# A sparse two-layer graph kernel: the first two same-lane slots summed ahead of TensorE, the bias as a matmul, and sorting held back

## The chip, the core and the metric

The kernel runs on one core of a Trainium2 chip. The core has five engines that run in parallel, each with its own queue of instructions in fixed order: TensorE (PE; its weight loads are listed apart as PEld), VectorE (DVE), ScalarE (ACT), GpSimd (POOL) and SyncE (SP). They wait for one another through semaphores. Data come from and go to the main memory by DMA, which SP, ACT and POOL issue. The metric is the device time of one execution in microseconds (us), as the median of several executions.

## What is computed

Two layers over a graph of 4096 nodes with 512 features. `adj` is a 4096 x 4096 matrix with some eight entries off the diagonal per row and a diagonal, all between 0.05 and 1; `x` is 4096 x 512.

```python
# layer 0
a = adj + I
d = sum(a, axis=1) ** -0.5
support = (d[:, None] * a * d[None, :]) @ x
h = layernorm(x + relu(support @ W.T + b))
# layer 1: attention over the entries of adj, with a mask value of 1e16
adj1 = maximum(adj, I)
scores = (q @ k.T) * kd ** -0.5 + 0.01 * I - 1e16 * (1 - adj1)
out = layernorm(h + softmax(scores) @ v @ Wo)       # 8 heads, summed
```

Where all entries of `adj` lie below 1, the mask leaves every row of layer 1 its own node alone, so that layer 1 is `layernorm(h + h @ Wv @ Wo)`, one product with a combined weight matrix `wvo`. The kernel tests this on the chip (`test`) and has a general path for the other case, which these inputs don't enter.

## The kernel before, in words

The 4096 rows are cut into NT = 32 tiles of 128. `few_edges_below_one` has two stages.

**First stage** (the loop from L1015). Each turn loads one 128 x 4096 tile of `adj` (2 MB), three turns ahead, over SP's queue; ScalarE sums its rows (`sum_rows`, L694) for the degree, GpSimd makes d from it (`scaling`, L706 to L709), TensorE transposes a tile of x and multiplies it by `wT` (`times`, L687), ScalarE scales the product by d (`keep_y`, L720) and GpSimd writes it to `y` in main memory. At the side VectorE turns each tile into a list of edges, a generator of small steps (`steps`) of which every turn takes RATE = 7 (`some`). A tile has 16 long steps, 8 MAX8 (L749) and 8 FIND_INDEX8 (L750), each over 512 columns: the eight largest entries of each eighth of a row and where they stand. Then some 30 short instructions (`short`) sort the 64 candidates of a row into at most 24 edges, with column and weight; those of one tile are mixed among the long steps of the next. `match` then moves the edges, over TensorE and a permutation, so that each row has KH = 9 slots (`cols_all`, `wr_all`).

EARLY = 12 tiles are scanned while they pass in the first stage, and their degree comes from the candidates (L935) and not from ScalarE. The last five tiles stay resident. The remaining 15 pass by once for their row sums in a small pool (`a_n`) and are loaded a second time in the second stage (`reload`) to be scanned. `order` is early, resident, again.

**Second stage** (the loop from L1246, tiles in `order`). For tile i and each slot k, GpSimd issues an indirect DMA that gathers the 128 rows of `y` that the edges name (`gather`, L1077) into a buffer `g`, 18 slots ahead of their use, in 19 buffers. ScalarE builds a 128 x 128 matrix per slot (`spread`) with the weights at the right places, and TensorE multiplies: nine products into one PSUM tile (`zs[i]`, L1280). In the first SAME = 5 slots every row keeps its lane, so that their matrices are one and the same 0/1 matrix (`s_t[:, KH]`, L983) times a weight per row (L986); the other four have one each (L973, L977). For the last two tiles (SUMMED) the five same-lane slots are summed first: ScalarE scales the first gathered tile by its weight (L1094), VectorE adds the others (`presum`, L1096), and one product with the 0/1 matrix takes the place of five (L1104).

VectorE then does `own_bias` (yo = yo * own + b, L1139, yo being the tile's own rows of `y`), `scaled` (h = zs * d + yo, L1146) and `residual` (relu and + x, L1154); ScalarE takes squares for the norms (L1162); TensorE transposes h (L673) two tiles later and multiplies by `wvo`; ScalarE scales by the last norm and issues the write of the result (L1185). The remaining scan and sort steps are dealt out over the first SPREAD = 28 tiles of this stage. ScalarE checks reloaded and resident tiles for negative entries, half a tile at a time (`scan_half`, L699); a reload waits for buffers that these halves and VectorE's scan set free. On SP's queue the reloads stand between the loads of `yo` and x, which wait for `scaled` and `residual` of three tiles before.

The order on each engine isn't that of the program text: a scheduler places the instructions, and the order is fixed when the program is built.

Of the kernel before, what the change touches and what calls it, by code (L numbers as in the profile page):

```python
# [419 lines left out]
def few_edges_below_one(  # L420
# [47 lines left out]
    recs = ctx.enter_context(tc.tile_pool(name="recs", bufs=8))  # L468
# [84 lines left out]
    EARLY, LAG = 12, 5  # L553
# [21 lines left out]
    b_bc = const.tile([P, D], FP, name="b_bc")  # L575
    wvo = const.tile([P, ND, D], FP, name="wvo")

    def transpose_w():
        for dc in range(ND):
            pt = ps_t.tile([P, 512], FP, name="pt")  # L580
            for oc in range(ND):
                nc.tensor.transpose(pt[:, ts(oc, P)], w_nat[:, oc, ts(dc, P)], ident)
            nc.scalar.copy(wT[:, dc, :], pt[:, :D])

# [143 lines left out]
    def extraction(t, a_t, rec):  # L728
# [6 lines left out]
        idx = keys.tile([P, C], U32, name="idx")  # L735
# [9 lines left out]
        long = []  # L745
        for s in range(SEGS):
            o = slice(s * E, (s + 1) * E)
            seg = a_t[:, ts(s, SW)]
            long.append(lambda o=o, seg=seg: nc.vector.max(v[:, o], seg))  # L749
            long.append(lambda o=o, seg=seg: nc.vector.max_index(idx[:, o], v[:, o], seg))  # L750
# [13 lines left out]
        def drop(f, r):  # L764
# [42 lines left out]
            [one(rec[:, 2], w, 0.0, row1n, op0=ALU.is_gt, op1=ALU.mult)],  # L807
# [7 lines left out]
        return long, short  # L815
# [103 lines left out]
    def steps():  # L919

        after = [[] for _ in range(STEPS)]
        for n, t in enumerate(order):
            if t not in a_tiles:
                reload()
            edges[t] = dict(rec=recs.tile([P, 7, K], FP, name="rec"))
            long, short = extraction(t, a_tiles[t], edges[t]["rec"])
            begun.append(t)
            for j in range(STEPS):
                long[j]()
                for f in after[j]:  # L930
                    f()
                if j == STEPS - 1:
                    picked.append(t)
                    if t in early:
                        nc.vector.tensor_reduce(  # L935
                            deg_all[:, t : t + 1], v_all[:, t, :], AX.X, ALU.add
                        )
                yield
            after = [[] for _ in range(STEPS)]
            for j, fs in enumerate(short):  # L940
                after[j] += fs
            after[len(short)].append(lambda t=t: sorted_.append(t))
        for fs in after:
            for f in fs:
                f()
            yield
# [19 lines left out]
    def spread(t, s_t, k, alone=False):  # L966


        wr = wr_all[:, t]

        def away():
            sq = mat.tile([P, P], FP, name="sq")
            nc.scalar.activation(sq, cols1, AF.Square, bias=wr[:, 2, k : k + 1])  # L973
            return sq

        if k >= SAME:
            nc.scalar.activation(  # L977
                s_t[:, k, :], away(), AF.Relu,
                scale=wr[:, 3, k : k + 1], bias=wr[:, 1, k : k + 1],
            )  # L980
            return
        if k == 0:
            nc.scalar.activation(s_t[:, KH, :], away(), AF.Relu, scale=-1.0, bias=1.0)  # L983
        if alone:
            return
        nc.scalar.activation(s_t[:, k, :], s_t[:, KH, :], AF.Copy, scale=wr[:, 1, k : k + 1])  # L986
# [4 lines left out]
    RATE = 7  # L991
# [21 lines left out]
    nc.gpsimd.dma_start(b_bc, bcast_rows(b0, D))  # L1013
    setup, left = iter(()), None
    for t in range(NT + 1):  # L1015
# [16 lines left out]
        for j in [j for at, j in due if at == t and j in early]:  # L1032
            scaling(j)
# [35 lines left out]
    SUMMED = (NT - 2, NT - 1)  # L1069
    slots = {}  # L1070
# [29 lines left out]
    def summed_products(i, pos, c=slice(0, D)):  # L1100

        k = SAME + pos if pos < KH - SAME else None
        g = slots[i * KH if k is None else i * KH + k]
        nc.tensor.matmul(  # L1104
            zs[i][:, c], mats[i][:, KH if k is None else k, :], g[:, c],
            start=(pos == 0), stop=(k is None),
        )

    def build(count):

        for _ in range(count):
# [5 lines left out]
            spread(order[i], mats[i], k, i in SUMMED)  # L1117
# [19 lines left out]
    def own_bias(i):  # L1137
        own = own_all[:, order[i] : order[i] + 1]
        nc.vector.scalar_tensor_tensor(yo[i], yo[i], own, b_bc, op0=ALU.mult, op1=ALU.add)  # L1139
# [3 lines left out]
    def scaled(i, c=slice(0, D)):  # L1143
        if i not in hs:
            hs[i] = p2.tile([P, D], FP, name="h", bufs=3)
        nc.vector.scalar_tensor_tensor(  # L1146
            hs[i][:, c], zs[i][:, c], d_all[:, order[i] : order[i] + 1], yo[i][:, c],
# [42 lines left out]
    def test():  # L1190
# [32 lines left out]
        [(i, k) for i in range(NT) for k in range(KH) if not (i in SUMMED and 0 < k < SAME)]  # L1223
# [22 lines left out]
    for i in range(NT + 2):  # L1246
        if i < NT:
            zs[i] = ps_a.tile([P, D], FP, name="acc")
        free = len([t for t in scanned if t in picked])
        p = i - 1  # L1250
        has_p = 0 <= p < NT
        for k in range(KH):
# [7 lines left out]
            if i == NT - 1:  # L1260
# [8 lines left out]
                if k == 8:  # L1269
                    for n in range(KH - SAME + 1):  # L1270
# [8 lines left out]
            elif i < NT:  # L1279
                nc.tensor.matmul(  # L1280
                    zs[i], mats[i][:, k, :], slots.pop(i * KH + k),
                    start=(k == 0), stop=(k == KH - 1),
# [4 lines left out]
            if i + 1 in SUMMED and k >= KH - SAME:  # L1287
                presum(i + 1, k - (KH - SAME))
# [26 lines left out]
            if k == 6 and i < NT:  # L1315
                own_bias(i)
# [48 lines left out]
```

## Time and profile before

| what | before |
|---|---|
| median of 3 runs | 649.07 us (648.53 to 650.29) |
| the profiled execution's own time | 647.33 us |
| its span, first to last instruction | 645.5 us |
| granted TensorE clock, mean | 0.944 of full speed |
| moved by DMA | 222.14 MB, mean 344 GB/s |
| gathers (L1077) | 288, 977 ns each on GpSimd, 7.3 us from issue to landing |
| products with gathered tiles (L1280) | 540 instructions for 270 products |
| scan (L749, L750) | 512 instructions, 687 and 691 ns each |
| own rows and bias (L1139) | 32, 743 ns each |
| matrices by scaling the 0/1 matrix (L986) | 150, 394 ns each |

The span is what the profiler saw between the first and the last instruction; the execution's own time has 1.8 us around it. Busy times are sums over an engine's records; on VectorE and ScalarE these overlap a little, so that the distance from one start to the next is the better measure of what an instruction costs in a full stretch.

### The profile page before, as it was taken

What the parts mean: (1) busy time and instruction counts of PE and PEld (TensorE: products, weight loads), DVE (VectorE), ACT (ScalarE), POOL (GpSimd) and SP (SyncE); (2) the same over time, 40 slices, a digit from 0 to 9 for tenths busy, and PEclk for the clock granted to TensorE, in tenths of its full rate; (3) what the DMA queues carried; (4) which work ended last, traced back from release to release, by engine and by line L of the source; (5) the groups of instructions that cost most, each with busy time, mean ns of one, the idle gap of its engine ahead of it and who ended that gap; (6) DMA issues with size and microseconds to landing.
All of it is one profiled execution on the core that took longest, in us unless ns stands there. A gap on an engine that the chain in (4) does not pass through costs nothing. (4 is left out here: it accounts for less than half of the span.)

```text
span 645.5 us, 7946 instructions
## 1 busy us (share of the span) xinstructions
PE 556.8 (86%) x1604; PEld 258.0 (40%) x1604; DVE 543.6 (84%) x2141; ACT 509.1 (79%) x1121; POOL 351.2 (54%) x464
## 2 busy tenths in 40 slices
PE   1698696888689486999999989999999999999794
PEld 1344342444244132444443434444444444444352
DVE  5679999999999994999999979999999996532431
ACT  1868888779779775999898957999979989994433
POOL 5132421323232377767666757766767777777700
PEclk9599998799879886999999989999999999999798
DMA  8999999999999289999999898999999988888721
GB/s 332 391 427 422 428 421 426 424 421 422 422 428 395 102 263 366 340 411 408 399 401 405 324 391 302 380 382 360 365 404 341 340 268 272 292 270 253 243 70 54
DMA packets 51850, 222.14 MB, mean 344 GB/s; under 512 B 8080, under 2 KB 9104, under 8 KB 45520
## 3 DMA queue, kind: packets, MB, share of 16 engines
q1 hardware_dynamic: 18416, 119.55, 45.6%
q0 software_dynamic: 28240, 92.56, 40.8%
q10 hardware_dynamic: 5136, 9.44, 3.8%
q14 instruction: 43, 0.35, 0.2%
q8 instruction: 15, 0.25, 0.2%
HBM read 204.73 MB, written 16.78 MB: 343 GB/s over the span
## 5 line engine op out<-in xcount | busy, mean ns | idle before, releaser
L1077 POOL DMA_INDIRECT g<-y,cols_all x288 | 281.4, 977 | 112.6 <-issue 41.9
L1280 PE MATMUL acc<-g,s_t 128*128 128x512 f32 x540 | 258.1, 612 | 23.8 <-DMA g<-y,cols_all 13.4
L749 DVE MAX8 v_all<-a_t 128x8 f32<-128x512 f32 x256 | 172.7, 687 | 16.9 <-DMA a_t<-in_adj_dram 16.9
L750 DVE FIND_INDEX8 idx<-v_all,a_t 128x8 uint32<-128x512 f32 x256 | 175.9, 691 | 0.0
L1280 PEld LDWEIGHTS acc<-g,s_t 128*128 128x128 f32 x540 | 98.0, 194 | 140.9 <-issue 92.8
L687 PE MATMUL acc<-wT,xT 128*128 128x512 f32 x256 | 126.6, 647 | 24.1 <-ACT xT L678 24.0
L699 ACT ACTIVATE dump<-a_t 128x2048 uint8<-128x2048 f32 (+1 forms) x52 | 119.5, 2299 | 4.4 <-DMA a_t<-in_adj_dram 4.3
L687 PE MATMUL acc<-wvo,hT 128*128 128x512 f32 x256 | 118.6, 606 | 5.0 <-ACT hT L678 4.6
L687 PEld LDWEIGHTS acc<-wT,xT 128*128 128x128 f32 x256 | 51.1, 207 | 86.9 <-issue 58.1
L687 PEld LDWEIGHTS acc<-wvo,hT 128*128 128x128 f32 x256 | 49.7, 196 | 67.4 <-issue 58.1
L973 ACT ACTIVATE sq<-cols,wr_all 128x128 f32<-128x128 f32 x160 | 58.1, 396 | 0.3 <-ACT hT L678 0.2
L694 ACT ACTIVATE dump<-a_n 128x4096 uint8<-128x4096 f32 x15 | 54.4, 3628 | 4.7 <-DMA a_n<-in_adj_dram 4.6
L977 ACT ACTIVATE s_t<-sq,wr_all 128x128 f32<-128x128 f32 x128 | 57.6, 487 | 0.5
L550 POOL DMA_DIRECT2D x_t<-in_x_dram x32 | 18.0, 562 | 68.1 <-PE pt L673 67.5
L986 ACT ACTIVATE s_t<-s_t,wr_all 128x128 f32<-128x128 f32 x150 | 48.9, 394 | 0.0
L1146 DVE SCALAR_TENSOR_TENSOR h<-acc,d_all,yo 128x512 f32<-128x512 f32 (+1 forms) x33 | 24.0, 727 | 20.9 <-PE acc L1280 15.9
L762 DVE MAX8 top<-key 128x8 f32<-128x64 f32 x192 | 41.0, 221 | 0.5
L678 ACT COPY hT<-pt 128x512 f32<-128x512 f32 x31 | 17.9, 579 | 23.8 <-PE pt L673 22.8
L706 POOL TENSOR_SCALAR deg<-deg_all 128x1 f32<-128x1 f32 x32 | 6.8, 224 | 48.0 <-ACT dump L694 47.9
L1139 DVE SCALAR_TENSOR_TENSOR yo<-yo,own_all,b_bc 128x512 f32<-128x512 f32 x32 | 23.8, 743 | 7.7 <-ACT own_all L1135 7.7
L673 PE MATMUL pt<-ident,x_t 128*128 128x128 f32 x128 | 20.3, 291 | 8.8 <-DVE above L841 7.6
L765 DVE MATCH_REPLACE8 key<-top,key 128x64 f32<-128x64 f32 x128 | 27.2, 214 | 0.0
(128 smaller groups left out, 643.5 us busy)
## 6 DMA issues: line engine op xcount, KB each, us to landing
a_t<-in_adj_dram SPq DMA_DIRECT2D x30, 2048.0 KB, 17.2
a_n<-in_adj_dram SPq DMA_DIRECT2D x15, 2048.0 KB, 17.4
x_t<-in_x_dram POOLq DMA_DIRECT2D x32, 256.0 KB, 11.9
yo<-y SPq DMA_DIRECT2D x32, 256.0 KB, 5.3
x_t<-in_x_dram SPq DMA_DIRECT2D x32, 256.0 KB, 5.6
out_dram<-r_t ACTq DMA_DIRECT2D x32, 256.0 KB, 6.4
g<-y,cols_all POOLq DMA_INDIRECT x288, 7.3
y<-y_t POOLq DMA_DIRECT2D x17, 256.0 KB, 11.9
```

Source lines behind the costliest of these rows:

```text
L687: nc.tensor.matmul(u, srcT[:, dc, :], w[:, dc, :], start=(dc == 0), stop=(dc == ND - 1))
L694: nc.scalar.activation(dump[:, : part.shape[1]], part, AF.Copy, accum_out=dst)
L699: nc.scalar.activation(dump[:, o], a_t[:, o], AF.Relu, scale=-1.0, accum_out=neg_all[:, t, halves[0] : halves[0] + 1],)
L749: long.append(lambda o=o, seg=seg: nc.vector.max(v[:, o], seg))
L750: long.append(lambda o=o, seg=seg: nc.vector.max_index(idx[:, o], v[:, o], seg))
L762: return lambda: nc.vector.max(top[:, f, r * 8 : r * 8 + 8], keyf[:, f])
L765: return lambda: nc.vector.match_replace(keyf[:, f], top[:, f, r * 8 : r * 8 + 8], keyf[:, f], 0.0)
L973: nc.scalar.activation(sq, cols1, AF.Square, bias=wr[:, 2, k : k + 1])
L977: nc.scalar.activation(s_t[:, k, :], away(), AF.Relu, scale=wr[:, 3, k : k + 1], bias=wr[:, 1, k : k + 1],)
L986: nc.scalar.activation(s_t[:, k, :], s_t[:, KH, :], AF.Copy, scale=wr[:, 1, k : k + 1])
L1077: nc.gpsimd.indirect_dma_start(out=slots[j], out_offset=None, in_=y[:, :], in_offset=bass.IndirectOffsetOnAxis(ap=cols_all[:, t, k : k + 1 ...
L1280: nc.tensor.matmul(zs[i], mats[i][:, k, :], slots.pop(i * KH + k), start=(k == 0), stop=(k == KH - 1),)
```

## The change

Four things, with what they bring along:

- *Two same-lane slots summed in tiles 1 to 29* (`summed`). ScalarE scales the first gathered tile by its weight, VectorE adds the second times its weight, and one product with the 0/1 matrix does for both. The two scaled matrices aren't built. Tile 0 stays as it was, and so do the last two tiles with five summed slots.
- *Bias on TensorE*. b is split into three bfloat16 parts that add up to it (`split_b`), and each tile begins with a small matmul of a 3 x 128 tile of ones with these (`bias`), which starts the sum in PSUM. For this the weights are multiplied by d as they are sorted (`one(w, w, d_all...)`), since zs is no longer scaled afterwards, and `scaled` becomes h = yo * own + zs. `own_bias` is gone.
- *Held sorting*. `extraction` is cut into `scan` (the long steps) and `sorting` (the short ones). Tiles wait in a list: the first five sorts run with the third to seventh scan (n = 2 to FULL = 6), none with n = 7 to 17, and from n = HELD = 18 on two with each scan until the list is empty. The index tiles get 15 buffers for this, the edge records 5 instead of 8.
- *Early tiles and rate*. EARLY is 14 instead of 12, so 13 tiles are reloaded instead of 15, and the first stage takes 9 steps a turn instead of 7. d of an early tile is computed as soon as its scan ends.

```diff
-    recs = ctx.enter_context(tc.tile_pool(name="recs", bufs=8))
+    recs = ctx.enter_context(tc.tile_pool(name="recs", bufs=5))
...
-    EARLY, LAG = 12, 5
+    EARLY, LAG = 14, 5
+    FULL, HELD = 6, 18
...
-    b_bc = const.tile([P, D], FP, name="b_bc")
+    b3 = const.tile([3, D], BF, name="b3")
+    ones3 = const.tile([3, P], BF, name="ones3")
+    nc.gpsimd.memset(ones3, 1.0)
...
+    def split_b():
+        t = [p1.tile([P, D], FP, name="x_t", bufs=6)[:3] for _ in range(3)]
+        nc.gpsimd.dma_start(t[0], bcast_rows(b0, D)[:3])
+        for n in range(2):
+            nc.vector.tensor_tensor(t[n + 1], t[n], t[n].bitcast(BF)[:, 1::2], ALU.subtract)
+        for n in range(3):
+            u, e = t[n].bitcast(BF)[:, 1::2], ident[:3, n : n + 1]
+            if n == 0:
+                nc.vector.tensor_scalar(b3, u, e, None, op0=ALU.mult)
+            else:
+                nc.vector.scalar_tensor_tensor(b3, u, e, b3, op0=ALU.mult, op1=ALU.add)
...
-    def extraction(t, a_t, rec):
+    def scan(t, a_t):
+        v = v_all[:, t, :]
+        idx = keys.tile([P, C], U32, name="idx", bufs=HELD - FULL + 3)
+        long = []
...
+        return long, idx
+
+    def sorting(t, idx, rec):
...
-            [one(rec[:, 2], w, 0.0, row1n, op0=ALU.is_gt, op1=ALU.mult)],
+            [
+                one(rec[:, 2], w, 0.0, row1n, op0=ALU.is_gt, op1=ALU.mult),
+                one(w, w, d_all[:, t : t + 1], None, op0=ALU.mult),
+            ],
...
+        waiting = []
+
+        def sort_some(count):
+            after = [[] for _ in range(STEPS)]
+            for t, idx in [waiting.pop(0) for _ in range(min(count, len(waiting)))]:
+                edges[t] = dict(rec=recs.tile([P, 7, K], FP, name="rec"))
+                short = sorting(t, idx, edges[t]["rec"])
+                for j, fs in enumerate(short):
+                    after[j] += fs
+                after[len(short)].append(lambda t=t: sorted_.append(t))
+            return after
+
         for n, t in enumerate(order):
...
-            long, short = extraction(t, a_tiles[t], edges[t]["rec"])
+            after = sort_some(0 if n < 2 or FULL < n < HELD else 1 if n <= FULL else 2)
+            long, idx = scan(t, a_tiles[t])
...
+                        scaling(t)
...
+            waiting.append((t, idx))
...
-        if alone:
+        if k == 0 and alone:
             return
...
-    RATE = 7
+    RATE = 9
...
+    summed = [1] + [2] * (NT - 3) + [SAME] * 2
...
-            spread(order[i], mats[i], k, i in SUMMED)
+            if k == 0 or k >= summed[i]:
+                spread(order[i], mats[i], k, summed[i] > 1)
...
-    def own_bias(i):
-        own = own_all[:, order[i] : order[i] + 1]
-        nc.vector.scalar_tensor_tensor(yo[i], yo[i], own, b_bc, op0=ALU.mult, op1=ALU.add)
+    def bias(i, c=slice(0, D)):
+        nc.tensor.matmul(zs[i][:, c], ones3, b3[:, c], start=True, stop=False)
...
-            hs[i][:, c], zs[i][:, c], d_all[:, order[i] : order[i] + 1], yo[i][:, c],
+            hs[i][:, c], yo[i][:, c], own_all[:, order[i] : order[i] + 1], zs[i][:, c],
...
             zs[i] = ps_a.tile([P, D], FP, name="acc")
+            bias(i, HALVES[0] if i == NT - 1 else slice(0, D))
...
-            elif i < NT:
+            elif i < NT and not 0 < k < summed[i]:
                 nc.tensor.matmul(
-                    zs[i], mats[i][:, k, :], slots.pop(i * KH + k),
-                    start=(k == 0), stop=(k == KH - 1),
+                    zs[i], mats[i][:, KH if k < summed[i] > 1 else k, :], slots.pop(i * KH + k),
+                    start=False, stop=(k == KH - 1),
                 )
...
-            if i + 1 in SUMMED and k >= KH - SAME:
-                presum(i + 1, k - (KH - SAME))
+            if i + 1 < NT and k >= KH - summed[i + 1] and summed[i + 1] > 1:
+                presum(i + 1, k - (KH - summed[i + 1]))
```

More of the change, by code (lines that the diff above doesn't have):

```diff
@@ L726, in upper @@
         return rec.bitcast(BF)[:, :, 1::2]
-    def extraction(t, a_t, rec):
+    def scan(t, a_t):
+        v = v_all[:, t, :]
+        idx = keys.tile([P, C], U32, name="idx", bufs=HELD - FULL + 3)
+        long = []
+        for s in range(SEGS):
+            o = slice(s * E, (s + 1) * E)
+            seg = a_t[:, ts(s, SW)]
+            long.append(lambda o=o, seg=seg: nc.vector.max(v[:, o], seg))
+            long.append(lambda o=o, seg=seg: nc.vector.max_index(idx[:, o], v[:, o], seg))
+        return long, idx
+    def sorting(t, idx, rec):
         v = v_all[:, t, :]
         vu = v.bitcast(U32)
-        idx = keys.tile([P, C], U32, name="idx")
         key = keys.tile([P, 2, C], U32, name="key")
@@ L744, in extraction @@
         home = slice(t // TS * E, (t // TS + 1) * E)
[L745 to L750, printed above, removed]
         def stt(out, a, sc, b, op0, op1, **kw):
@@ L814, in extraction @@
         ]
-        return long, short
+        return short
     second = []
@@ L919, in steps @@
     def steps():
-        after = [[] for _ in range(STEPS)]
+        waiting = []
[8 more added lines that the diff above has]
+            return after
         for n, t in enumerate(order):
@@ L924, in steps @@
                 reload()
-            edges[t] = dict(rec=recs.tile([P, 7, K], FP, name="rec"))
-            long, short = extraction(t, a_tiles[t], edges[t]["rec"])
+            after = sort_some(0 if n < 2 or FULL < n < HELD else 1 if n <= FULL else 2)
+            long, idx = scan(t, a_tiles[t])
             begun.append(t)
@@ L937, in steps @@
                         )
+                        scaling(t)
                 yield
[L939 to L943, printed above, removed]
+            waiting.append((t, idx))
+        for fs in sort_some(len(waiting)):
             for f in fs:
@@ L1012, in few_edges_below_one @@
     transpose_w()
-    nc.gpsimd.dma_start(b_bc, bcast_rows(b0, D))
+    split_b()
     setup, left = iter(()), None
@@ L1031, in few_edges_below_one @@
         got = begin() if kind == "t" else None
-        for j in [j for at, j in due if at == t and j in early]:
-            scaling(j)
         if t < NT:
@@ L1105, in summed_products @@
             zs[i][:, c], mats[i][:, KH if k is None else k, :], g[:, c],
-            start=(pos == 0), stop=(k is None),
+            start=False, stop=(k is None),
         )
@@ L1222, in few_edges_below_one @@
     to_build = iter(
-        [(i, k) for i in range(NT) for k in range(KH) if not (i in SUMMED and 0 < k < SAME)]
+        [(i, k) for i in range(NT) for k in range(KH)]
     )
@@ L1269, in few_edges_below_one @@
                 if k == 8:
+                    bias(i, HALVES[1])
                     for n in range(KH - SAME + 1):
@@ L1314, in few_edges_below_one @@
                 variance(t)
-            if k == 6 and i < NT:
-                own_bias(i)
             if k == 6 and has_p:
```

## The prediction

> **What bounds the kernel now.** I read the page first, then the busy time by stretches, then the groups by shape, then the instructions of TensorE and VectorE in order of time, and last the order in which each engine's instructions stand in the two built programs.
>
> ```profile
> span 645.5 us, 7946 instructions
> ...
> PE 556.8 (86%) x1604; PEld 258.0 (40%) x1604; DVE 543.6 (84%) x2141; ACT 509.1 (79%) x1121; POOL 351.2 (54%) x464
> ```
> ```profile
> 20.00:40.00 20.00, 16.96 (x49) 9.12 (x49) 14.44 (x60) 12.70 (x13) 4.96 (x7) 0.73 1.02 403
> 240.00:260.00 20.00, 13.81 (x27) 5.32 (x28) 10.90 (x41) 12.17 (x34) 15.26 (x15) 0.74 0.93 335
> 300.00:320.00 20.00, 19.26 (x53) 8.45 (x52) 19.38 (x81) 18.12 (x51) 13.99 (x15) 1.00 1.03 410
> 500.00:520.00 20.00, 20.00 (x60) 9.21 (x59) 20.00 (x85) 16.27 (x49) 15.41 (x16) 1.00 0.96 338
> 540.00:560.00 20.00, 20.00 (x59) 9.34 (x58) 9.19 (x39) 19.40 (x57) 15.42 (x16) 1.00 0.86 281
> ```
> (Columns: the stretch, its length, busy time of PE, PEld, DVE, ACT and POOL, clock, DMA share, GB/s.) The reader is to see that the average of 84 to 86% hides one long stretch, from 260 to 540 us, in which TensorE and VectorE are both full, and that VectorE alone has room before 60, in 240 to 260 and after 540.
>
> ```profile
> L1077 POOL DMA_INDIRECT g<-y,cols_all x288 | 281.4, 977 | 112.6 <-issue 41.9 <-DMA g<-y,cols_all 29.1 <-PE acc L1280 26.0
> L1280 PE MATMUL acc<-g,s_t 128*128 128x512 f32 x540 | 258.1, 612 | 23.8 <-DMA g<-y,cols_all 13.4 <-DMA yo<-y 9.6 <-ACT s_t L977 0.2
> L750 DVE FIND_INDEX8 idx<-v_all,a_t 128x8 uint32<-128x512 f32 x256 | 175.9, 691 | 0.0
> L749 DVE MAX8 v_all<-a_t 128x8 f32<-128x512 f32 x256 | 172.7, 687 | 16.9 <-DMA a_t<-in_adj_dram 16.9
> L1139 DVE SCALAR_TENSOR_TENSOR yo<-yo,own_all,b_bc 128x512 f32<-128x512 f32 x32 | 23.8, 743 | 7.7 <-ACT own_all L1135 7.7
> ```
> ```profile
> 521.68 5.32 PE L1280 MATMUL acc<-g,s_t 128*128 128x512 f32 x12
> 526.83 3.60 PE L687 MATMUL acc<-wvo,hT 128*128 128x512 f32 x8
> 530.27 2.74 PE L1280 MATMUL acc<-g,s_t 128*128 128x512 f32 x6
> 532.84 0.27 PE L832 MATMUL pt<-ident,rank_key 128*128 128x128 f32 x1
> 532.95 0.60 PE L673 MATMUL pt<-ident,h 128*128 128x128 f32 x4
> 533.39 3.60 PE L1280 MATMUL acc<-g,s_t 128*128 128x512 f32 x8
> ```
> Tile 23 of the second stage: a product is two instructions; six of them take 526.83-521.68 = 5.15 us, so one is 0.858. Nine products, four more for the output weights (3.43), transposes and edge moves make 11.8 us a tile, back to back from 480 to 592. GpSimd's gathers follow each other every 1.255 us when nothing holds them (223.25 to 258), so nine cost 11.3 us.
>
> ```profile
> 504.11 0.09 DVE L750 MATCH_VALUE_LOAD idx<-v_all,a_t 128x8 f32 x1
> 504.18 0.69 DVE L750 FIND_INDEX8 idx<-v_all,a_t 128x8 uint32<-128x512 f32 x1
> 504.78 0.20 DVE L1173 TENSOR_SCALAR sums<-sums 128x1 f32<-128x1 f32 x1
> ```
> VectorE's records overlap; start to start FIND_INDEX8 with its load is 0.665, MAX8 0.60, a 512-wide three-operand instruction 0.61 to 0.66, a small one 0.1 to 0.2. The scaled rows (L1146) start at 257.50 (tile 1), 525.65 (tile 22) and 538.47 (tile 23): 281 us for 22 tiles, 12.8 each, on an engine that is full. So the kernel stands between two bounds: VectorE near 12.6 a tile, TensorE 11.8.
>
> [...] PE read 19.3 of 20 at 300 us with gaps for gathers inside, and kept 11.8 a tile once VectorE thinned out. [...] half of the 0.43 of one fp32 instruction here, so the bfloat16 bias is estimated at 0.22 us. [...] the trace has 743 (L1139) and 752 (L1096), and these are used.
>
> **The change, part by part.**
> *TensorE.* Tiles 1 to 29 lose one product, 29 x 0.858 = 24.9 us; 33 bias matmuls add about 7. If a bias costs as much as an fp32 pass, 0.43, it is 14; if weight load and clock hide it, nothing. It matters only after VectorE has let go, eight times, so the ends are -2 and +2 us. Per tile 11.8 becomes 11.2, about the gathers' 11.3.
> *VectorE totals.* Away: 32 own-plus-bias rows (L1139). New: 29 presums of the same form (0.66), 32 multiplications of a 128x24 weight row by d (about 0.15, 5 us), five 3-row splits of b (2 to 3 us), two degree sums. A 128x24 operation of that kind stands in the trace at 0.256 long and 0.14 to 0.18 apart (L759, weight row times row number), so 32 of them cost 4.5 to 8; a rewritten scaled row (yo times own plus PSUM) has the same operands in another order and is taken as equal, 0.66. The sum is +3 to +8 us: the engine that is full gets no relief.
> *ScalarE.* 58 copies of 0.31 go (L986: five in 1.56), 29 scalings of 0.60 come: even.
> *Earlier scanning.* Two more early tiles, 9 steps instead of 7 a load, sorting held. I laid the start-to-start times along VectorE's order (the sum for before, 220, is raised 0.6% to its busy time of 221.2 at tile 0's scaled row, 239.15). The changed order has 57 more scan steps and 6 sorts fewer there: 235. The waits shrink: before, VectorE waits 5.8, 1.2, 5.4 (tile 2) and 3.9 (tile 4); now its second tile is tile 1, landed near 21 us (ScalarE sums it at 20.6), its third tile 3 (about 39, one 6.0 us load before tile 4 at 45.4), with sorts and the split of b between: 8.2 in all instead of 17.2. So tile 0's scaled row stands at 244.
> *The new wait.* The first product of every tile from 1 on waits for VectorE's presum, which waits for ScalarE's scaling and two gathers. Behind it on TensorE stand the tile's other seven products and the output product of tile i-2; for those wait scaled rows and slot releases. Tile 1: presum done at 245.5, eight products, 252.6 (before 257.3, held by gathers). The first reload sits on SP behind yo(3), which waits for scaled(0): issued about 246.5, some 10 us to land (before: issued 241.07, data moving to 250), 256.5, when VectorE has run out of sorts. Then 19.3 us of queue stand between scaled(1) and scaled(2): 272.7, against 269.44 before. Presum(2) is inside it, so TensorE idles some 8 us there.
> *The long stretch.* From scaled(2) to presum(23) the order holds 247 us; before, a like stretch of 254 took 256.2, so 249 here: 521.7. The same place before, tile 23's first product, was 521.68. So nine tiles from the end the two kernels are level: TensorE has given its lead back to VectorE.
> *The end.* There VectorE is free and TensorE sets the pace: 123.8 us remained before; 7 x (0.858-0.22) = 4.5 go, 0.4 of bias comes in the last two tiles. At 598 TensorE waited 4.6 us for a copy of ScalarE queued behind the scaling of a gather not yet there; with slots now full 19 ahead this may go or stay (0 to 4.6, half taken). 117.4 remain: a span of 639.1. The profiled execution took 647.33 for 645.5, and the median of the runs is 1.74 above it: 639.1+1.8+1.7 = **643**.
> Two fewer reloads (4 MB) are costed at nothing: DMA isn't last anywhere after 260; GpSimd's floor, 223.25+288x1.255+34.5 to the end = 619, isn't reached.
>
> **Rivals.**
> A, VectorE doesn't hold: if ScalarE's and VectorE's queues run ahead, GpSimd's floor decides: 619+3.6 = 623. For it: the load of TensorE really falls. Against: VectorE's sum of 12.6 a tile through tile 22.
> B, slower: TensorE and VectorE are now locked once a tile. VectorE's order puts presum(i+1) some 10 us after scaled(i-1), and ScalarE's scaling is queued behind its square of tile i-1, the edge row of a match and sometimes a 1.9 us half scan, which I add to about 8 us after scaled(i-1); twice the gap is only 6.6. Each us that VectorE stands there in tiles 2 to 22 is 21 us at the end. It decides from (649-643)/21 = 0.3 us a tile; at 0.6 the time is 655. For it: the margin. Against: the gathers run 19 ahead, and ScalarE has 1 us a tile to spare.
> C, level: the early waits don't shrink (split of b waiting for x buffers, a later tile 1) and 5 us come back: 648.
> That the change isn't made can be left out: the built program has 241 products for 270 and 37 presums for 8.
>
> **How the numbers follow.** About 0.3%, 2 us, is what a measurement can tell from no change: faster is under 647.1, slower over 651.0. Chances: forecast 0.53 (635 to 647), A 0.12, B 0.23, C 0.12. Faster 0.65, same 0.12, slower 0.23. The range takes the forecast, C and the near half of B: 635 to 656.
>
> **What would show it.** Right: VectorE without gaps from 257 to about 525, scaled(0) near 244, TensorE idle in small pieces before its first product of a tile (waiting for g of VectorE), tiles 11.2 apart after 525. Wrong: presums waiting for ScalarE's g (B), scaled(0) near 250 (C), TensorE gapless before 500 (A).

## The result, and the profile after

The changed kernel takes 646.11 us (median of six runs, 645.29 to 647.21); the kernel before, run beside it, took 650.64 (648.53 to 651.9). The ratio is 0.9932, 95% interval 0.9911 to 0.9954: faster by 0.7%, where 643 was forecast. The two profiled executions differ by much less, 646.95 against 647.33, because the profiled one of before lies below its other runs; a few us between these two traces are therefore no measure of the gain, and positions in them are compared place by place instead.

The page's head and first part:

```profile
span 645.2 us, 7918 instructions
...
PE 545.8 (85%) x1579; PEld 251.2 (39%) x1579; DVE 546.0 (85%) x2143; ACT 504.6 (78%) x1114; POOL 352.8 (55%) x465
```

TensorE's busy time fell by 11.0 us, VectorE's rose by 2.4. The busy time by stretches, in the columns used before (stretch, length, PE, PEld, DVE, ACT, POOL, clock, DMA share, GB/s):

```profile
20.00:40.00 20.00, 16.97 (x52) 9.17 (x53) 15.69 (x54) 11.92 (x12) 5.79 (x9) 0.91 1.03 407
240.00:260.00 20.00, 12.21 (x26) 4.91 (x24) 12.17 (x71) 12.13 (x34) 14.72 (x16) 0.91 0.84 286
300.00:320.00 20.00, 16.87 (x47) 7.57 (x48) 18.92 (x88) 20.00 (x57) 14.67 (x15) 0.91 1.02 390
400.00:420.00 20.00, 20.00 (x59) 8.98 (x58) 18.76 (x93) 14.64 (x44) 15.29 (x16) 0.96 0.93 314
500.00:520.00 20.00, 20.00 (x64) 9.10 (x63) 19.98 (x93) 19.46 (x59) 15.16 (x16) 1.00 0.84 266
540.00:560.00 20.00, 20.00 (x60) 8.90 (x59) 9.54 (x38) 19.84 (x59) 15.12 (x17) 1.00 0.87 293
```

At 300 TensorE has room, 16.87 of 20 where it had 19.26 before; from 400 on it is full again although it has less to do. The groups by shape and, for TensorE's waits, the list of what each engine waited for (total us, times, longest):

```profile
L1110 POOL DMA_INDIRECT g<-y,cols_all x288 | 282.5, 981 | 107.1 <-issue 43.1 <-DMA g<-y,cols_all 24.0 <-PE acc L1316 19.4
L1316 PE MATMUL acc<-g,s_t 128*128 128x512 f32 x482 | 232.0, 618 | 28.0 <-DVE g L1129 17.1 <-DMA x_t<-in_x_dram 10.9
L752 DVE MAX8 v_all<-a_t 128x8 f32<-128x512 f32 x256 | 166.3, 677 | 8.2 <-DMA a_t<-in_adj_dram 8.2
L1129 DVE SCALAR_TENSOR_TENSOR g<-g,wr_all 128x512 f32<-128x512 f32 x37 | 27.5, 743 | 25.5 <-ACT g L1127 22.7 <-DMA g<-y,cols_all 2.6
```
```profile
PE acc L1316 <- DVE g L1129: 17.1, 8, 4.7
```

The products are 58 records fewer (29 products), VectorE's sums are 37 for 8, its waits for adjacency loads fell from 16.9 to 8.2 us. The new wait is the last of these lines: eight times TensorE stood before a tile's first product until VectorE had summed the first two slots, once 4.7 us (tile 1), the others 2.4 at most, seven of the eight before 400 us.

One turn of TensorE, in order of time (L1173 is the bias product, L689 the transposes of a finished tile, L1316 the products):

```profile
492.08 0.27 PE L856 MATMUL pt<-ident,rank_key 128*128 128x128 f32 x1
492.29 0.39 PE L1173 MATMUL acc<-b,ones 3*128 3x512 bf16 x1
492.60 0.66 PE L689 MATMUL pt<-ident,h 128*128 128x128 f32 x4
493.09 2.74 PE L1316 MATMUL acc<-g,s_t 128*128 128x512 f32 x6
...
504.14 0.66 PE L689 MATMUL pt<-ident,h 128*128 128x128 f32 x4
```

From the transposes of one tile to those of the next are 504.14 - 492.60 = 11.54 us, without a gap. From 410 to 596 sixteen turns take 185.5 us, 11.6 each, with one wait of 0.65 for a sum.

Before 410 the pace is another. From tile 2 to tile 12 the scaled rows (L1180, h = yo * own + zs) come every 13.3 us, longer than TensorE's turn. The stretch from 275 to 410 us, before and after, in the columns used above:

```profile
275.00:410.00 135.00, 128.79 (x371) 57.00 (x370) 129.71 (x503) 117.58 (x330) 92.37 (x96) 0.99 0.99 379
275.00:410.00 135.00, 122.14 (x354) 54.02 (x353) 130.07 (x587) 120.84 (x331) 95.83 (x98) 0.97 1.01 387
```

VectorE is nearly full there (130.07 of 135), but so are the DMA engines, with a busy share of 0.99 and 1.01. Which of the two sets the pace up to tile 12 is not shown by this profile.

### The profile page after: what moved, and what is told of

Read it like the earlier page. It is cut to its first block, busy times and chain, and to the rows that moved or that the text cites. A ratio compares the mean times of both kernels' runs of the same rounds, so it can differ in the third digit from the quotient of the medians.

```text
span 645.2 us, 7918 instructions
## 1 busy us (share of the span) xinstructions
PE 545.8 (85%) x1579; PEld 251.2 (39%) x1579; DVE 546.0 (85%) x2143; ACT 504.6 (78%) x1114; POOL 352.8 (55%) x465
## 5 line engine op out<-in xcount | busy, mean ns | idle before, releaser
L1316 PE MATMUL acc<-g,s_t 128*128 128x512 f32 x482 | 232.0, 618 | 28.0 <-DVE g L1129 17.1
L752 DVE MAX8 v_all<-a_t 128x8 f32<-128x512 f32 x256 | 166.3, 677 | 8.2 <-DMA a_t<-in_adj_dram 8.2
L1316 PEld LDWEIGHTS acc<-g,s_t 128*128 128x128 f32 x482 | 89.8, 196 | 125.9 <-issue 95.1
L1129 DVE SCALAR_TENSOR_TENSOR g<-g,wr_all 128x512 f32<-128x512 f32 x37 | 27.5, 743 | 25.5 <-ACT g L1127 22.7
L710 ACT ACTIVATE dump<-a_n 128x4096 uint8<-128x4096 f32 x13 | 47.3, 3636 | 0.0
L1127 ACT ACTIVATE g<-g,wr_all 128x512 f32<-128x512 f32 x31 | 22.1, 713 | 24.0 <-DMA g<-y,cols_all 16.8
L783 DVE MAX8 top<-key 128x8 f32<-128x64 f32 x192 | 36.0, 213 | 0.3
L1180 DVE SCALAR_TENSOR_TENSOR h<-yo,own_all,acc 128x512 f32<-128x512 f32 (+1 forms) x33 | 23.8, 720 | 11.2 <-PE acc L1316 7.8
L1020 ACT ACTIVATE s_t<-s_t,wr_all 128x128 f32<-128x128 f32 x92 | 33.0, 391 | 0.0
L694 ACT COPY xT<-pt 128x512 f32<-128x512 f32 x32 | 18.3, 594 | 11.5 <-PE pt L689 11.5
```

Of the source, the lines that this page charges most:

```text
L694: copy = nc.scalar.copy(dst.rearrange("p c s -> p (c s)"), pt[:, :D])
L710: nc.scalar.activation(dump[:, : part.shape[1]], part, AF.Copy, accum_out=dst)
L783: return lambda: nc.vector.max(top[:, f, r * 8 : r * 8 + 8], keyf[:, f])
L1316: nc.tensor.matmul(zs[i], mats[i][:, KH if k < summed[i] > 1 else k, :], slots.pop(i * KH + k), start=False, stop=(k == KH - 1),)
```

## The experiments

The first four kernels ran together on one chip, with the kernel before at 650.84 us. The change has three parts: the schedule (14 early tiles, 9 steps a load, sorting held), the sums of two slots by VectorE, and the bias on TensorE. The four runs take them apart. The fifth to twelfth run follow the first stage and met other chips.

**Without the sums**

```diff
-    summed = [1] + [2] * (NT - 3) + [SAME] * 2
+    summed = [1] * (NT - 2) + [SAME] * 2
```

> The changed kernel (646.1 us) with the summing by VectorE undone in tiles 1 to 29: those tiles have nine products again, bias on TensorE and the new order of scans and sorts stay. Theory (two engines in turn: VectorE's queue sets the pace to about 400 us, TensorE from there): a tile on TensorE becomes 11.55 + 0.86 = 12.4 us, which is then the slower of the two everywhere, the 17.1 us of waits for VectorE's sum vanish, tile 23's first product comes near 526 as in the changed kernel, and the rest costs 7 x 0.86 = 6 us more: 651 to 653. Rival (the lock of TensorE to VectorE's sum costs more than the product saves): without the 17 us of waits the time falls to 636 to 642.

Measured: 656.5 us (654.52 to 657.23), ratio to before 1.0093 (1.0065 to 1.0121). The rival falls; the theory has the direction, but sized the loss too low: tile 23's first product comes at 531.42, not near 526, and only 3.8 us more than in the changed kernel lie behind it, not 6. In this kernel's tile on TensorE, late in the second stage, the transposes follow each other every 12.40 us:

```profile
505.81 0.38 PE L1173 MATMUL acc<-b,ones 3*128 3x512 bf16 x1
506.12 0.66 PE L689 MATMUL pt<-ident,h 128*128 128x128 f32 x4
506.62 3.60 PE L1316 MATMUL acc<-g,s_t 128*128 128x512 f32 x8
...
518.52 0.66 PE L689 MATMUL pt<-ident,h 128*128 128x128 f32 x4
```

12.40 - 11.54 = 0.86 is the price of a product, as forecast. VectorE has 18.8 us less to do than in the changed kernel (527.2 against 546.0), and nothing is gained by that. From tile 12 on, where a tile takes 12.4 us, TensorE sets the pace alone. Up to tile 12 it doesn't: a tile takes 13.3 us there (scaled rows at 274.36 and 407.59), as in the changed kernel, although no tile waits for a sum and VectorE has less to do.

```profile
275.00:410.00 135.00, 133.17 (x392) 57.76 (x391) 127.97 (x585) 120.67 (x343) 91.85 (x95) 1.00 0.99 376
```

The DMA engines' share is 0.99 here too, and 1.00 in the three kernels below, at 12.7 to 13.0 us a tile. A bound set by the loads and gathers together in this stretch would fit all six kernels; no run tests it.

**Bias back on VectorE**

```diff
-    split_b()
+    nc.gpsimd.dma_start(b_bc, bcast_rows(b0, D))
...
-    def bias(i, c=slice(0, D)):
-
-        nc.tensor.matmul(zs[i][:, c], ones3, b3[:, c], start=True, stop=False)
+    def own_bias(i):
+        own = own_all[:, order[i] : order[i] + 1]
+        nc.vector.scalar_tensor_tensor(yo[i], yo[i], own, b_bc, op0=ALU.mult, op1=ALU.add)
...
-            hs[i][:, c], yo[i][:, c], own_all[:, order[i] : order[i] + 1], zs[i][:, c],
-            op0=ALU.mult, op1=ALU.add,
+            hs[i][:, c], zs[i][:, c], 1.0, yo[i][:, c], op0=ALU.mult, op1=ALU.add,
...
+            if k == 6 and i < NT:
+                own_bias(i)
```

With the bias products the split of b into three rows goes too, so that this run and the one of the schedule alone also change the first stage (see below).

> The changed kernel with the bias back on VectorE (yo times own plus b, one 0.66 us instruction a tile more) and no bias product on TensorE; everything else stays. Theory: VectorE's queue is the bound to about 400 us, so 11 to 14 tiles pay 0.66 each, 7 to 9 us, and the 16 to 18 tiles after it gain 0.41 each, about 7 us: level to slightly slower, 645 to 650, with more waits of TensorE for the sum. Rival (TensorE paces all along): 33 x 0.41 = 13 us gained, 633 to 636.

Measured: 647.49 us (642.08 to 651.01), ratio 0.9951 (0.993 to 0.9973): not to be told from the changed kernel, as the theory had it. TensorE is relieved (533.8 us busy) and waits for VectorE instead. Its waits, same list as above:

```profile
PE acc L1298 <- DVE g L1114: 30.5, 13, 9.8
```

13.4 us more than in the changed kernel stand in this one line, and the 33 bias products had kept TensorE busy for 12.1: the two sums nearly match. So TensorE's relief shows as waiting; that the one became the other is inferred from these sums.

**The old schedule**

```diff
-    recs = ctx.enter_context(tc.tile_pool(name="recs", bufs=5))
+    recs = ctx.enter_context(tc.tile_pool(name="recs", bufs=8))
...
-    EARLY, LAG = 14, 5
+    EARLY, LAG = 12, 5
...
-        idx = keys.tile([P, C], U32, name="idx", bufs=HELD - FULL + 3)
+        idx = keys.tile([P, C], U32, name="idx", bufs=3)
...
-            after = sort_some(0 if n < 2 or FULL < n < HELD else 1 if n <= FULL else 2)
+            after = sort_some(1)
...
-    RATE = 9
+    RATE = 7
```

> The changed kernel with the old schedule of VectorE's work (12 early tiles, 7 steps a load, each tile sorted during the scan of the next); the sums by VectorE and the bias product stay. Theory: the first product comes some 4 us earlier (no dip in the loads of the first stage), but some 57 scan steps of about 0.63 us, less six sorts, come back into the long stretch where VectorE is full: the first product of tile 23 falls to 532 to 538, and with 117.5 us from there the time is 650 to 656, no faster than before the change. Rival (the schedule is worth nothing or costs, because the dip in the first stage eats it): 642 to 646.

Measured: 648.15 us (645.33 to 654.98), ratio 0.9957 (0.9933 to 0.9981). Neither expectation holds: the schedule is worth less here than the theory had it, and the first gather came not earlier than in the changed kernel but later, at 230.51. VectorE is full longer, as the theory had it (40.00 of 40 in 500 to 540, against 35.44), but tile 23's first product comes at 529.34, not at 532 to 538: from the first gather to it are 298.8 us, against 301.2 in the changed kernel. So the scan steps that came back did not delay tile 23 as forecast.

**The schedule alone**

The two edits of the first and second run together.

> The changed kernel with both other parts undone: nine products a tile, bias on VectorE, only the new order of scans and sorts (and the weights multiplied by d in the sort, 32 small VectorE instructions). Theory: TensorE has 12.0 us a tile and VectorE's relief in the second stage lets it run at that; first product about 233, tile 23 near 520, rest 124: span 644, time 645 to 648, so most of the gain is in the schedule alone. Rival (the gain is the removed product): as before the change, 650 to 652.

Measured: 646.5 us (643.21 to 651.78), ratio 0.9948 (0.9929 to 0.9968). That is the changed kernel's gain within the intervals: the sums and the bias on TensorE add nothing that can be measured to the new schedule, and without it they give 0.9957. The parts do not add up. The sums and the bias move work between TensorE and VectorE, as the busy times show (PE, DVE in us): before 556.8 and 543.6; schedule alone 551.3 and 543.9; schedule and bias 565.0 and 527.2; schedule and sums 533.8 and 559.9; sums and bias 543.8 and 549.3; all 545.8 and 546.0. The kernel with TensorE at 565 is slower than before; the others lie together, from 0.9932 to 0.9957.

The time was as expected, but not its parts: 523.24 for tile 23's first product, later than expected and later than before (521.68), and 119.7 us from there instead of 124.

```profile
523.24 3.17 PE L1298 MATMUL acc<-g,s_t 128*128 128x512 f32 x7
```

This trace also shows the price of the bias. Its tile:

```profile
510.76 0.27 PE L841 MATMUL pt<-ident,rank_key 128*128 128x128 f32 x1
510.87 0.60 PE L674 MATMUL pt<-ident,h 128*128 128x128 f32 x4
511.31 3.60 PE L1298 MATMUL acc<-g,s_t 128*128 128x512 f32 x8
...
522.81 0.60 PE L674 MATMUL pt<-ident,h 128*128 128x128 f32 x4
```

The period is 11.94, with nine products and no bias, against 12.40 with nine products and bias: a bias product costs 0.46 us. The two kernels with eight products say the same: 11.54 with the bias, 11.08 without (transposes at 406.81 and 417.89 in the run with the bias on VectorE). Start to start it takes 0.31 (506.12 - 505.81); the transpose ahead of it takes 0.21 to the next start where it took 0.11 (492.29 - 492.08 against 510.87 - 510.76), and the four behind it 0.50 where they took 0.44. Here the short instruction is paid for in its neighbours as well.

**The first stage.** The first gather starts at 223.25 before, at 226.55 in the changed kernel and 225.0 in the one without the sums, but at 220.84 and 221.03 in the two kernels with b on VectorE. The kernels that split b into three bfloat16 rows on the new schedule start 4 to 6 us later than those that don't. (On the old schedule the split goes with a first gather at 230.51; why it is so late there was not taken apart.) VectorE's records of the changed kernel show the start of it, and the page's row of GB/s by fortieths of the span (first the changed kernel's, then that of the schedule alone) the dip that the next run traces back to it:

```profile
25.01 0.47 DVE L597 TENSOR_SCALAR b<-x_t,ident 3x512 bf16<-3x512 bf16 x1 [4.01 <-DMA x_t<-in_L_gnn_b_dram]
```
```profile
GB/s 331 402 421 421 424 428 423 286 422 424 423 425 419 157 270 284 400 351 385 387 408 409 401 401 387 305 348 348 328 362 280 269 263 300 281 285 276 238 70 54
```
```profile
GB/s 330 394 428 420 426 422 428 421 428 425 421 427 408 129 271 318 367 354 404 409 400 390 387 382 327 373 366 352 304 329 296 255 275 291 270 299 256 247 80 54
```

VectorE stands 4.01 us for the load of b; GpSimd's queue, in which the loads of x stand, waits 6.1 us for the split to give its buffers back (three of the six of x). The eighth figure of the row, about 113 to 129 us, is 286 with the split and 421 without.

**The split apart.** The next kernel takes the split apart from the rest.

```diff
-        t = [p1.tile([P, D], FP, name="x_t", bufs=6)[:3] for _ in range(3)]
+        t = [wvo[:3, n] for n in range(3)]
         nc.gpsimd.dma_start(t[0], bcast_rows(b0, D)[:3])
+        yield
...
-    split_b()
+    split = split_b()
+    next(split)
...
         some((t + 1) * RATE)
+        if t == 2:
+            next(split, None)
```

> The changed kernel (646.1 us) with the split of b staged in the memory of wvo, which is written much later, instead of in three of the six buffers of the loads of x, and with VectorE's five small instructions of it issued after the third tile's share of scans instead of before the first. Theory (the split holds VectorE 4 us at 25 us and the loads of x behind it, which ends as a dip in the adjacency loads at 120 to 140 and a later first gather; both kernels with b on VectorE have it at 221.0 and 220.8, those with the split at 225.0 to 230.5): no wait for b, no dip, first gather near 221, time 640 to 643. Rival (the dip comes from the new order of scans, and the end is set by VectorE's sum of work anyway): first gather stays at 224 to 227, time 645 to 647.

The first gather came at 220.64, and the dip is gone: 415 GB/s from 100 to 140 us where the changed kernel has 368. For the first stage that is what the theory said and the rival denied. Two things changed together, the memory and the place of the instructions in the queues; which of them counts is not separated. The time says nothing on the rest: 714.47 us, where the kernel before took 684.22 beside it. This was another chip, and there the second stage of each kernel traced is slower; more on it below. The ratio there is 1.042 (1.0371 to 1.0469).

Three kernels built on this one ran on the same chip. The bias products left out:

```diff
-            start=False, stop=(k is None),
+            start=(pos == 0), stop=(k is None),
...
-            bias(i, HALVES[0] if i == NT - 1 else slice(0, D))
...
-                    bias(i, HALVES[1])
...
-                    start=False, stop=(k == KH - 1),
+                    start=(k == 0), stop=(k == KH - 1),
```

> As the kernel with the split of b apart, but the 33 bias products are left out (the bias is missing from the result; the split of b is still made). Theory (a bias product costs TensorE 0.41 us a tile where TensorE sets the pace, from about 400 us, 18 tiles, and nothing before): tiles from 400 on come every 11.14 us if VectorE follows; VectorE's 12.0 to 12.2 a tile up to tile 22 takes some of that back, so 3 to 6 us less than the kernel with the bias products: 635 to 640. Rival (0.22 us each, or hidden): at most 2 us less.

Measured: 717.39 us, ratio 1.0475 (1.043 to 1.0521): no gain at all where TensorE has gaps (it is busy for 339.44 of the 440 us from 220 to 660). The expectation was written for a chip where before takes about 650 and isn't tested by this. VectorE's sums only from tile 12 on:

```diff
-    summed = [1] + [2] * (NT - 3) + [SAME] * 2
+    summed = [1] * 12 + [2] * (NT - 2 - 12) + [SAME] * 2
```

> As the kernel with the split of b apart, but VectorE sums the first two slots only from tile 12 on (tiles 1 to 11 have nine products again). Theory (VectorE sets the pace through tile 12 and its sum of work decides when tile 23 begins): 11 instructions of 0.66 us less in that queue, 7 us, and none of the eight waits of TensorE for the sum before tile 12; tile 23 starts 5 to 7 us earlier, time 4 to 6 us under the kernel with the split apart: 635 to 639. Rival (TensorE's sum decides): 11 x 0.86 = 9.5 us more products, time 2 to 9 us longer: 644 to 652.

Measured: 716.86 us, ratio 1.0474 (1.0422 to 1.0526), an interval that overlaps that of the kernel with the split apart; the theory's gain of 4 to 6 us does not show. The sums sooner:

```diff
-            if i + 1 < NT and k >= KH - summed[i + 1] and summed[i + 1] > 1:
-                presum(i + 1, k - (KH - summed[i + 1]))
+            if i + 1 < NT and summed[i + 1] > 1:
+                at_k = k - (KH - summed[i + 1] - (3 if summed[i + 1] == 2 else 0))
+                if 0 <= at_k < summed[i + 1]:
+                    presum(i + 1, at_k)
```

> As the kernel with the split of b apart, but the scaling by ScalarE and the sum by VectorE of the next tile's first two slots stand three slots earlier in the queues, by about a third of a tile. Theory (the 17 us of TensorE's waits for the sum are only VectorE's lateness seen from TensorE): the waits change hands, the time falls by 0 to 2 us: 639 to 642. Rival (the lock itself costs): the waits vanish and the time falls by 5 to 12 us: 630 to 637.

Measured: 705.25 us, ratio 1.0309 (1.026 to 1.0358), 1.3% under the kernel with the split apart. On this chip, where VectorE stands still at unforeseen places (47 us in 26 gaps without a releaser in the trace of the kernel with the split apart), sums issued a third of a tile sooner do pay; TensorE's waits for them fall from 64.2 to 51.2 us.

Two of these were tried again and met a third chip like the second.

> The kernel with the split of b apart once more, since on the chip of its first run the kernel before took 684 us and VectorE stood 47 us in gaps that no event explains. Where the kernel before takes about 650: theory (the split caused the dip in the first stage) first gather near 221, ratio to before 0.985 to 0.989, 640 to 643; rival (the first stage doesn't decide, VectorE's sum of work does) first gather near 221 all the same, ratio 0.992 to 0.995, as the changed kernel.

> The same with VectorE's sums only from tile 12 on, once more for the same reason. Theory (VectorE's queue sets the pace through tile 12): tile 23 starts 5 to 7 us earlier than in the kernel with the split apart, ratio lower by 0.006 to 0.009. Rival (TensorE's sum decides): tile 23 later, ratio higher by 0.003 to 0.014.

Measured: 716.32 and 721.55 beside a kernel before of 687.67, ratios 1.0421 (1.0383 to 1.0458) and 1.0461 (1.0404 to 1.0518). First gather 221.25. The first expectation's condition, a kernel before near 650, was not met. The sums from tile 12 on are again not faster; twice their ratio is the higher one, by 0.005 and 0.004, as the rival had it, but within the intervals; tile 23's first product is level in the first pair of traces (585.03 and 585.85) and 8.0 us later in the second (593.13 and 585.11).

**The changed kernel on such a chip**

That left open whether the edit or the chip made these kernels slow. The four groups of runs were each on a chip of their own, so "chip" here means the chip and the hour at which it was used. The last two runs, on a fourth chip, were the changed kernel unaltered and, beside it, the one with the split apart and the sums sooner.

> The changed kernel itself, unaltered. On two chips the kernel before took 684 to 688 us and every kernel derived from the changed one 3 to 5% more than it. Where before takes about 650: ratio 0.991 to 0.996 as first measured. Where before takes about 685: if those kernels were slow because of the chip, the changed one has the same gaps of VectorE beside GpSimd's gathers and a ratio of 1.03 to 1.05; if it was the staging of b in wvo or the late split, its ratio stays at 0.99 to 1.00.

> The split of b apart and the sums three slots sooner, once more, beside the changed kernel on one chip. Theory (the split costs 5 us of the first stage, the waits for the sum are mostly VectorE's lateness): first gather near 221, where before takes 650 a ratio to it of 0.983 to 0.988, 4 to 7 us under the changed kernel. Rival (the lock itself costs): the waits for the sum fall from 17 us to under 5 and the time is 9 to 14 us under the changed kernel.

Measured: 723.15 us (720.71 to 728.74), ratio 1.0515 (1.0458 to 1.0573), and 711.82 (707.08 to 718.26), ratio 1.0329 (1.0272 to 1.0386); before took 689.13. So the edits of the split and of the sums are not what made those kernels slow: where the kernel before takes about 689, the changed kernel itself is 5% slower than it, not 0.7% faster. The two mends together take 11.3 us off the changed kernel there (711.82 against 723.15, ranges apart), 3.7 us of which its first gather shows (221.49 against 225.22). The gain has the size that the rival gave, without its sign: the waits for the sum are 51.6 us, not under 5. For the split apart alone there is only a comparison across chips, of ratios to before: 1.042 twice, against 1.0515 for the changed kernel.

Where the time goes on that chip, the changed kernel's trace tells only in part. Up to the first gather (225.22) it runs as in the first measurement (226.55). Then VectorE stops between small instructions of a sort, with no instruction in the trace as releaser ("remote" and "issue" in the brackets):

```profile
250.13 0.18 DVE L835 TENSOR_TENSOR rec<-rec 128x24 f32<-128x24 f32 x1 [2.73 <-remote]
251.52 0.18 DVE L835 TENSOR_TENSOR rec<-rec 128x24 f32<-128x24 f32 x1 [1.21 <-remote]
252.92 0.09 DVE L753 MATCH_VALUE_LOAD idx<-v_all,a_t 128x8 f32 x1 [1.22 <-remote]
...
258.49 0.23 DVE L774 SCALAR_TENSOR_TENSOR key<-v_all,place 128x64 uint32<-128x64 uint32 x1 [1.17 <-issue]
262.02 0.23 DVE L774 SCALAR_TENSOR_TENSOR key<-v_all,key 128x64 uint32<-128x64 uint32 x1 [3.30 <-remote]
```
```profile
PE acc L1316 <- DVE g L1129: 65.2, 10, 27.3
```

The trace of the first measurement has the last two of these 0.14 us apart (243.51, 243.65). Such gaps sum to 49 us on VectorE here and to none there: 19 before tile 0's scaled row, which comes at 267.76 instead of 246.84, 11 from there to 620 us, and 19 after that, where VectorE has idle time anyway. The first group accounts for most of the 21 us by which that row is late; where the other 56 us of the loss arise is not shown. A slower TensorE is not the reason: the granted clock was 0.896 in the mean, against 0.946, but the two instructions of a product start 0.429 us apart (the median) in both traces.

TensorE stood 65.2 us for the sums, against 17.1 (last line above). That the loss reaches the end through this wait is not shown. With the sums only from tile 12 on, the waits for them are 11.4 and 10.3 us on the second and third chip, where they are 64.2 and 62.9 with the split apart alone, and the time is no shorter. After 225 us TensorE's idle time is 82.8 and 82.7 us there, against 93.4 and 93.2; the difference is about what eleven more products take (9.4). TensorE then stands at other places, for instance 6.04 us at 548.06 on the third chip for a rank key (`rank_key`, a small operand of `match`) from ScalarE.

## Why the prediction was right, and where it was not

**The direction and its reason.** It was forecast that VectorE, the full engine, gets no relief from the moved work, and that the gain is only what earlier scanning and TensorE's shorter tiles leave. The first half is shown: VectorE's busy time is 546.0 against 543.6. The second is not. The schedule alone gives 0.9948, but its trace has tile 23 no earlier than before, and its 4.2 us lie behind that place; the sums and the bias without the schedule give 0.9957, with 5.7 us more on VectorE than before. VectorE's sum of work does not set the time by itself.

**Earlier scanning: a wait left out.** Tile 0's scaled row was put at 244 and stands at 246.84. The work up to there was put at 235 us, and VectorE was busy for 234.1. Its early waits were put at 8.2 us; the waits for adjacency loads came to 8.2, and the 4.01 for the load of b came on top. That is the place that rival C named, with 5 us as its price.

**The first stage: not in the sum.** The gathers were taken to start where they had, at 223.25; they start at 226.55. The prediction costed the five instructions of the split at 2 to 3 us of VectorE and left out the buffers of x that it holds. With the split apart it is 220.6 to 221.9 in seven traces, on other chips, where the unaltered kernel has 225.22: the step cost about 4 us there, and 4 to 6 where before takes about 650.

**The new wait.** The sum of tile 1 was put at 245.5 and starts at 247.51; tile 1's scaled row at 252.6, and is at 257.00; the first reload at 246.5, and is issued at 249.27; tile 2's scaled row at 272.7, and is at 276.97. Each is late, by 2.0 to 4.4 us, about as much as tile 0's scaled row (2.8) and the gathers' start (3.3) before them; how much comes from which was not taken apart. The order was right. The idle time of some 8 us before tile 2's first product did not come as one piece: TensorE stood 4.75 us for tile 1's sum, 3.32 for a rank key and 1.89 for a copy of h, the last two from ScalarE.

**The long stretch.** 249 us were forecast from tile 2's scaled row to tile 23, and 527.73 - 276.97 = 250.8 were measured. That the total fits is in part luck, for the pace within it was not seen: 13.3 us a tile up to tile 12 and 12.0 after, and TensorE all but gapless from 410 on. "TensorE gapless before 500" was to be the sign of rival A; it came without A's time, since TensorE's own tile was longer than forecast. Tile 23's first product was put at 521.7 and stands at 527.73, the 4.3 us by which tile 2's row was late and the 1.8 of this stretch.

**DMA, costed at nothing.** "DMA isn't last anywhere after 260" doesn't hold for the kernel before: in 275 to 410 its TensorE stood 6.1 us, in nine pieces, for gathers to land. With a DMA share of about 1 in that stretch in all six kernels traced where before takes about 650, the price of reloads there stays open.

**The price of the bias: a term too small.** A tile was put at 11.2 and takes 11.54. The bias was taken at 0.22, half of the 0.43 of one fp32 instruction; the half was the author's estimate, shown by no trace. The upper bound named was 0.43. Measured are 0.31 from its start to the next and 0.46 in the tile. So the estimate was too low for this product among fp32 work, and the measured price counts.

**The end.** 117.4 us were forecast from tile 23 on and 117.5 were measured. That is luck in part: the bias products took 7 x 0.24 = 1.7 us more, and of the ScalarE wait of 4.58, half of which was kept in the sum, 1.47 are left at 602.56, and 0.49 in one more place, 0.3 less than kept. The other 1.3 us or so that make up for the bias are not accounted for.

```profile
527.73 2.74 PE L1316 MATMUL acc<-g,s_t 128*128 128x512 f32 x6
602.64 2.93 PE L687 MATMUL acc<-wvo,hT 128*128 128x512 f32 x3 [4.58 <-ACT hT L678]
602.56 1.98 PE L703 MATMUL acc<-wvo,hT 128*128 128x512 f32 x4 [1.47 <-ACT hT L694]
```

(The first line is tile 23's first product in the changed kernel, the second the wait before, the third the wait after.)

**The sum.** A span of 639.1 was forecast and 645.2 measured, all of it before tile 23. To the span 1.8 and 1.7 were added for the median; the second of these belonged to one execution of before, and the changed kernel's profiled execution lies 0.84 above its median. These two, and 0.4 of rounding, hide part of the miss: an error of 6.1 us in the span shows as 3.1 in the time. In the two traces alone nearly nothing is gained (645.5 and 645.2); the gain of 4.5 us is one of the medians.

**Rivals.** B, the lock of TensorE to VectorE's sum, exists (17.1 us in eight waits) but does not decide in the first measurement. Its sign was sums that wait for ScalarE's scaling, and VectorE has such waits:

```profile
DVE g L1129 <- ACT g L1127: 22.7, 6, 7.9
273.49 0.75 DVE L1129 SCALAR_TENSOR_TENSOR g<-g,wr_all 128x512 f32<-128x512 f32 x1 [0.71 <-ACT g L1127]
```

Only this one of the six, 0.71 us, lies in tiles 2 to 22; the others come from 536 us on, where VectorE has room. All of VectorE's waits from 258 to 525 sum to less than 6 us. (That the kernel without sums is slower, 656.5, says less, since it has 29 products more.) On the fourth chip the waits for the sum are 65.2 us; they can't be counted as the loss of 77, as said above. A did not come: TensorE's tile is 11.54 against 11.3 for nine gathers, and GpSimd waited 24.0 us for earlier gathers to land and 19.4 for TensorE, so that its floor was not reached.

Open: the kernels with the split apart were not timed on a chip like the first. From its first gather, 5.7 us earlier in the kernel with the schedule alone, some 5 us may be had; that is argued, not shown, and the kernel with the bias on VectorE, whose first gather is 5.5 us earlier, was no faster than the changed one. Open too are what sets the pace up to tile 12, and why the kernel before loses only 38 us on the fourth chip and the changed one 77; before was not traced there.

## What to carry to other kernels

Where two engines are full side by side, moving work from one to the other can be worth nothing, as here (0.9932 with the moves, 0.9948 without): add up each engine's busy time for each part of a change by itself, and expect the parts not to add. Look at the DMA share of the same stretch (here 0.99 to 1.01 from 275 to 410 us) before calling an engine the bound. Setup work for a small operand can cost more than its own instructions, through the buffers or the queue places that it borrows: here 4 to 6 us of the first gather for instructions of 2.9. A wait that ties two engines once a tile shows where one of them is late; whether it costs anything is shown only by taking it away, and here the waits fell from 64.2 and 62.9 us to 11.4 and 10.3, TensorE stood at other places, and the time was no shorter.

## What the runs showed of the hardware

- The same program took 646 us in the first measurement and 723 on the fourth chip, the kernel before about 650 in two measurements and 684 to 689 on three other chips. The changed kernel's first 225 us were alike (first gather at 226.55 and 225.22); the difference begins once GpSimd's gathers run, which go out every 1.25 us (the median) in both traces. VectorE then stands without a releaser in the trace 26 times, 0.3 to 5.1 us each, 49 us in all, against none in the first measurement. The cause is not settled.
- A bfloat16 product with three weight rows among fp32 work cost 0.46 us (a turn of 12.40 with it, 11.94 without), 0.31 of it to the next start and the rest in the transposes around it.
- The granted clock's mean was 0.896 on the fourth chip against 0.946 in the first measurement, and yet the two instructions of a product started 0.429 us apart (the median) in both.
